# Moving the q terms behind the third head's transposes, and taking every turned probability off PSUM with ScalarE

## The chip, the cores and the metric

The kernel runs on one core of a Trainium2 chip. TensorE (PE, with its weight loads shown apart as PEld) multiplies and transposes and writes to the banks of PSUM; VectorE (DVE) and ScalarE (ACT) read those banks; GpSimd (POOL) works on SBUF alone; SyncE (SP) issues the DMAs. The metric is the device time of one execution in microseconds. Of three runs before the change the median was 2974.68 us (2971.85 to 2978.81).

## The reference

It is one transformer block: adaptive layer norm, attention with relative positions in both q and k, and a mixture of experts. Sixteen batches of 512 rows, 256 wide, 16 heads of 16 columns, all float32.

```python
scores = jnp.einsum('bhqd,bhkd->bhqk', q, k)
dist_idx = pos_l - pos_r + M - 1          # below 0 it wraps, past the end it clamps
pos_emb = dist_emb[dist_idx]
rel_q = jnp.einsum('bhld,lrd->bhlr', q, pos_emb)
rel_k = jnp.einsum('bhrd,lrd->bhlr', k, pos_emb)
probs = softmax((scores + rel_q + rel_k) / sqrt(D))
ctx = einsum('bhqk,bhkd->bhqd', probs, v)
h = layernorm(ctx @ Wo + bo + hidden_states) * ln_gamma + ln_beta
x = x + ga * h
# then: layer norm, modulation, router, top 2 of 8 experts, sum of their outputs, residual
```

`rel_q` and `rel_k` cost the most. They are computed apart from the scores, block by block, written to DRAM, and read back as the start value of the scores.

## The kernel before

A prologue normalizes the input, projects q, k and v, and computes the first ten blocks of relative terms. Then come 64 units. A unit is one tile of 128 query rows of one batch; it handles its 16 heads in four groups (g = 0 to 3) of four heads each. Beside its own attention a unit does parts of other work: the block of relative terms that is needed ten units later (q terms in the unit itself, k terms from its last slots into the next unit), and the tail of earlier units (projection, layer norm, routing, experts). The last ten units have no such block to compute.

The order is written out by hand. A unit is 16 slots, four for each group; `at(slot, order, fn, ...)` files a piece of work under a slot and an order in it, and the last loop of the kernel emits everything by slot and order. The tile context is in manual-schedule mode, so each engine's queue is exactly that order; the framework adds the semaphores and gives out the buffers. What stands in a group's four slots on TensorE, with the names used later:

- slot 0: the first head's four transposes (`turn`, line 669, tile pt), then the next group's scores (`content`, line 644, tile qk, one bank for each of four heads). In g = 0 the expert biases (line 821, fpb) follow.
- slot 1: the second head's transposes, in g = 1 two more of the tail (line 719, pct), then the context product of the group before (line 687, pc), then the q terms (`q_set`, line 165, tile pq, four banks), in g = 3 the router (line 791, fpl).
- slot 2: the third head's transposes, then a pair of experts (line 830, fpy).
- slot 3: the k terms (`k_set`, line 186, tile pk, four banks), the fourth head's transposes, and one more piece of the tail: line 702 (pcl), 730 and 735 (ph), 778 (fpt) or 813 (fpmt), for g = 0 to 3.

One call of `q_set` is 8 matmuls, each on 32 rows of the array, so that four of them run side by side, and each of the four row groups has a bank of its own; the profile has two records for each matmul. The k terms and the scores work in the same way.

Who reads the banks: VectorE adds the scores to the relative terms and takes the maximum (line 650), adds the k terms in place (line 195), copies the first head's transposes (line 674) and takes one expert of each pair (line 841). ScalarE copies the transposes of the second to fourth head (line 672) and the q terms (line 175), does the exponentials (line 660, two heads in slot 2 and two in slot 3, for the next group), and the other expert of a pair (line 845, ye). All TensorE output but the context's goes through one pool of seven banks (`ps`, tag g), and a tile waits until the last reader of the bank it gets is done. In the program's own order a tile mostly gets the bank that was used seven tiles before.

Of the kernel before, what the change touches and what calls it, by code (L numbers as in the profile page):

```python
# [34 lines left out]
def adaln_attention_moe_kernel(  # L35
# [34 lines left out]
    nc = tc.nc  # L70
# [51 lines left out]
    def bank(name):  # L122
        return ps.tile([P, S], F32, tag="g", name=name)


    class Rel:
# [7 lines left out]
        @staticmethod  # L134
        def at(n):
            s, m = n // 32, n % 32
            return s, m // 8, m % 8 // 2, m % 2
# [70 lines left out]
    rel = Rel()  # L208


    with ExitStack() as pro:
# [205 lines left out]
        with tc.tile_pool(name="setup", bufs=1) as su:  # L417
# [34 lines left out]
            for cc in range(NE):  # L452
                pt = bank(f"scT_{cc}")[:, 0:NB]
# [207 lines left out]
                t_["s", g][:, t, :], t_["s", g][:, t, :], AF.Exp, bias=t_["m", g][:, t : t + 1]  # L661
            )

    def turn(u, g, t, on_act):
        t_ = units[u]
        pt = bank(f"pt_{u}_{g}_{t}")
        for rb in range(NL):
            cols = slice(rb * P, (rb + 1) * P)
            nc.tensor.transpose(pt[:, cols], t_["s", g][:, t, cols], ident)  # L669
        pT = tp.tile([P, S], F32, tag="pT", name=f"pT_{u}_{g}_{t}")  # L670
        if on_act:
            nc.scalar.copy(pT, pt)  # L672
        else:
            nc.vector.tensor_copy(pT, pt)  # L674
        t_["p", g, t] = pT

    def context(u, g):
# [190 lines left out]
    for u in range(NP):  # L868
        z = 16 * u
        for g in range(4):  # L870
            q0 = z + 4 * g
            at(q0 - 12, 0, load_scores, u, g)
            at(q0 - 4, 5, content, u, g)
            at(q0 - 2, 7, exps, u, g, (0, 1))
            at(q0 - 1, 7, exps, u, g, (2, 3))
            for t in range(4):
                at(q0 + t, 3, turn, u, g, t, t > 0)
            at(q0 + 5, 4, context, u, g)
        at(z - 16, 0, lambda u: units.setdefault(u, {}), u)
        at(z - 13, 0, load_k, u, 0)  # L880
        at(z - 6, 0, load_k, u, 1)
        at(z - 15, 0, load_q, u)
        at(z - 7, 0, mask_q, u)
        at(z - 9, 0, load_rest, u)
        at(z + 15, 0, load_tail, u)
        z += 16
        at(z + 3, 6, back, u)
        at(z + 5, 3.5, contextT, u)
        at(z + 7, 6, project, u)
        at(z + 8, 0, residual, u)  # L890
        at(z + 10, 0, norm2, u)
        at(z + 11, 6, modulate, u)
        at(z + 13, 7, route, u)
        at(z + 15, 7, mask_t, u)
        at(z + 16, 7, bias, u)
        for pr in range(4):
            at(z + 18 + 4 * pr, 6, experts, u, pr)
            at(z + 19 + 4 * pr, 1, expert_sums, u, pr)
        at(z + 35, 0, finish, u)

        z -= 16
        n = u + LEAD
        if n < NP:
            for g in range(4):
                at(z + 1 + 4 * g, 6, rel.q_set, n, g)
                at(z + 15 + 4 * g, 2, rel.k_set, n, g)
            for g in range(4):
                at(z + 28 + 2 * g, 0, rel.store, n, g)
        if n + 1 < NP:
            for w in rel.wants(n + 1):  # L910
                o = 8 + w[3] if w[0] == "q" else (16, 17, 21, 25)[w[2] % 2 * 2 + w[3]]
                at(z + o, 0, rel.load, w)
# [52 lines left out]
```

## Time and profile before

| | before |
|---|---|
| median of 3 runs | 2974.68 us |
| profiled execution | 2971.56 us |
| its span, first to last instruction | 2969.8 us |
| TensorE clock granted, mean | 0.971 |
| distance of units that compute q terms | 40.05 us |
| distance of most of the last ten units | 28.5 us |
| DMA moved over the span | 268 GB/s |

The span is divided so: some 500 us of prologue, about 2120 us with units that also compute relative terms, the rest with units that don't. In the middle of the run the granted clock is full. A record of TensorE ends where the profile models its end, so records can be longer than the work in them; the chain of waits follows the last instruction back to what held it, and gives the time between one end and the next.

### The profile page before, as it was taken

To read this page: it belongs to the slowest core of one execution; us is meant where nothing else is said; L and a number is where in the kernel's file an instruction comes from. 1 tells how busy PE (TensorE), PEld (TensorE's weight loads), DVE (VectorE), ACT (ScalarE), POOL (GpSimd) and SP (SyncE) were. 2 spreads that over 40 slices of the span, in tenths; PEclk is the share of its full clock that TensorE was granted. 3 is DMA by queue.
4 is the path that set the end of the run, shared out by engine and by line. 5 is a ranking of instruction groups with operands and counts; after the bars stand their busy time and mean duration, and the time that the engine had idled before them with its cause. 6 is when DMAs were issued, how large, how long until landed. Compare 5 with 4: busy or idle time off the path is not lost.

```text
span 2969.8 us, 75984 instructions
## 1 busy us (share of the span) xinstructions
PE 2815.0 (95%) x30186; PEld 1845.8 (62%) x30186; DVE 1984.0 (67%) x5396; ACT 1933.7 (65%) x3682; POOL 629.8 (21%) x863
## 2 busy tenths in 40 slices
PE   8889864999999999999999999999999999999997
PEld 5556552666666666666666666666666666666564
DVE  5446542777777777777767777677777767776664
ACT  2344433777776777777677677777767777767774
POOL 1000000121222222122222212222222222222333
PEclk9889866999999999999999999999999999999999
DMA  6879997798988889988888998888898888898661
GB/s 191 302 260 319 298 302 259 229 290 268 287 269 271 280 283 293 280 272 281 272 271 277 287 281 274 268 283 277 281 295 268 286 273 272 272 280 279 211 232 54
DMA packets 855346, 796.46 MB, mean 268 GB/s; under 512 B 25545, under 2 KB 649409, under 8 KB 854737
## 3 DMA queue, kind: packets, MB, share of 16 engines
q1 hardware_dynamic: 854032, 790.03, 84.3%
q8 instruction: 240, 3.93, 0.5%
q10 hardware_dynamic: 960, 1.57, 0.2%
q14 instruction: 114, 0.93, 0.1%
HBM read 462.20 MB, written 328.25 MB: 266 GB/s over the span
## 4 chain that ended last, share of the span: by engine, by line
PE 79%; POOL 2%; DMA 1%; DVE 1%; SPq 1%; issue 1%; ACT 1%; POOLq 0%; ACTq 0%; DVEq 0%
PE pt L669 18%; PE fpy L830 14%; PE pq L165 13%; PE qk L644 12%; PE pc L687 8%; PE pk L186 8%; PE ph L735 2%; PE fpl L791 1%; PE pcl L702 1%; POOL qm L614 1%; DMA vu<-v_d 1%; PE fpt L778 1%; PE fpb L821 0%; PE pct L719 0%; POOL rstd L101 0%
## 5 line engine op out<-in xcount | busy, mean ns | idle before, releaser
L175 ACT COPY r<-pq 128x512 f32<-128x512 f32 x1024 | 525.4, 603 | 385.8 <-PE pq L165 368.9
L195 DVE TENSOR_TENSOR r<-pk,r 128x512 f32<-128x512 f32 x1024 | 635.0, 683 | 192.8 <-PE pk L186 187.3
L660 ACT ACTIVATE s<-s,mx 128x512 f32<-128x512 f32 x1024 | 691.6, 735 | 50.2 <-DVE mx L654 47.2
L650 DVE CUSTOM_DVE_ANT_0 s<-qk,s 128x512 f32<-128x512 f32 x1024 | 644.0, 685 | 39.2 <-PE qk L644 36.7
L669 PE MATMUL pt<-ident,s 128*128 128x128 f32 x4096 | 652.0, 283 | 10.7 <-ACT s L660 10.3
L669 PEld LDWEIGHTS pt<-ident,s 128*128 128x128 f32 x4096 | 451.0, 142 | 289.3 <-issue 77.7
L672 ACT COPY pT<-pt 128x512 f32<-128x512 f32 x768 | 459.5, 598 | 252.1 <-PE pt L669 250.4
L851 POOL TENSOR_TENSOR ye<-ye,ye 128x256 f32<-128x256 f32 x192 | 140.6, 732 | 1633.0 <-ACT ye L845 1627.5
L830 PE MATMUL fpy<-we_sb,fhT 128*128 128x512 f32 x1024 | 483.4, 595 | 0.0
L165 PE MATMUL pq<-t_r,qe 32*128 32x256 f32 x4096 | 467.1, 417 | 4.0 <-DMA qe<-eq_d 2.9
L644 PE MATMUL qk<-k,qm 32*128 32x512 f32 x2048 | 388.9, 644 | 28.0 <-POOL qm L614 28.0
L186 PEld LDWEIGHTS pk<-t_f,ke 32*128 32x128 f32 x8192 | 268.8, 190 | 189.1 <-ACT pT L672 157.7
L841 DVE SCALAR_TENSOR_TENSOR fy<-fpy,fmask,fy 128x256 f32<-128x256 f32 x256 | 123.8, 483 | 384.6 <-PE fpy L830 375.6
L165 PEld LDWEIGHTS pq<-t_r,qe 32*128 32x128 f32 x4096 | 283.3, 186 | 143.1 <-DVE mx L650 67.8
L186 PE MATMUL pk<-t_f,ke 32*128 32x128 f32 x8192 | 321.2, 288 | 7.2 <-DVE r L195 3.4
L687 PE MATMUL pc<-pT,vu 128*32 128x128 f32 x8192 | 278.2, 277 | 0.0
L830 PEld LDWEIGHTS fpy<-we_sb,fhT 128*128 128x128 f32 x1024 | 175.4, 191 | 124.9 <-issue 124.9
L687 PEld LDWEIGHTS pc<-pT,vu 128*32 128x32 f32 x8192 | 209.2, 110 | 43.5 <-issue 42.9
L644 PEld LDWEIGHTS qk<-k,qm 32*128 32x128 f32 x2048 | 141.5, 183 | 104.6 <-DVE r L195 47.3
L674 DVE COPY pT<-pt 128x512 f32<-128x512 f32 x256 | 174.5, 682 | 24.9 <-PE pt L669 20.3
L101 POOL TENSOR_TENSOR rstd<-rstd,mhalf 128x1 f32<-128x1 f32 (+1 forms) x144 | 88.0, 611 | 438.5 <-DVE rstd L100 434.9
L845 ACT ACTIVATE ye<-fpy,fmask 128x256 f32<-128x256 f32 x256 | 127.5, 498 | 45.2 <-DVE fy L841 45.1
(111 smaller groups left out, 2175.6 us busy)
## 6 DMA issues: line engine op xcount, KB each, us to landing
rel_d<-r SPq DMA_DIRECT2D x256, 1024.0 KB, 8.5
s<-rel_d SPq DMA_DIRECT2D x256, 1024.0 KB, 7.8
vu<-v_d SPq DMA_DIRECT2D x64, 576.0 KB, 7.7
ke<-ek_d SPq DMA_DIRECT2D x128, 256.0 KB, 7.1
k<-k_d SPq DMA_DIRECT2D x128, 256.0 KB, 6.5
gt<-gates_d SPq DMA_DIRECT2D x64, 256.0 KB, 4.7
v_d<-v SPq DMA_DIRECT2D x16, 576.0 KB, 6.4
xt<-in_x SPq DMA_DIRECT2D x16, 512.0 KB, 6.1
```

The source lines that it names most:

```text
L165: nc.tensor.matmul(bs[t][:, a * 256 : (a + 1) * 256], e[32 * t : 32 * t + 32, (g % 2) * 2 + a, :], t_r[32 * t : 32 * t + 32, :, m0 : m0 + RK],
L175: nc.scalar.copy(dst[:, t], bs[t].rearrange("p (a c) -> p a c", a=2))
L186: nc.tensor.matmul(bs[t][:, a * 128 : (a + 1) * 128], e[32 * t : 32 * t + 32, a, :], t_f[32 * t : 32 * t + 32, :, m0 : m0 + LQ], start=Tru ...
L195: nc.vector.tensor_tensor(dst, bs[t].rearrange("p (r l) -> p l r", r=8), dst, ALU.add)
L644: nc.tensor.matmul(bs[t], t_["q"][rows, pa, cc, :], t_["k", cc][rows, :], start=True, stop=True)
L650: nc.vector.tensor_tensor_reduce(st[:, t, :], bs[t], st[:, t, :], 0.25, -3.0e38, ALU.add, ALU.max, mx[:, t : t + 1],)
L660: nc.scalar.activation(t_["s", g][:, t, :], t_["s", g][:, t, :], AF.Exp, bias=t_["m", g][:, t : t + 1])
L669: nc.tensor.transpose(pt[:, cols], t_["s", g][:, t, cols], ident)
L672: nc.scalar.copy(pT, pt)
L674: nc.vector.tensor_copy(pT, pt)
L687: nc.tensor.matmul(pc[32 * t : 32 * t + 32, g, :], t_["v"][:, rb, h * VW : h * VW + 32], pTs[t][:, rb * P : (rb + 1) * P], start=(rb == 0) ...
L830: nc.tensor.matmul(py, t_["hT"][:, kc, :], we_sb[:, kc, pr * 2 * E : (pr + 1) * 2 * E], start=(kc == 0), stop=(kc == NE - 1),)
```

## The change

The q terms of a group move from slot 1, order 6 to slot 2, order 4: from behind the context product to behind the third head's transposes (order 3 in slot 2) and ahead of the experts (order 6). The copy of the first head's transposes moves from VectorE to ScalarE, so that `turn` has one form for all four heads. With that, the pool gives out its banks in another order.

```diff
-    def turn(u, g, t, on_act):
+    def turn(u, g, t):
...
         pT = tp.tile([P, S], F32, tag="pT", name=f"pT_{u}_{g}_{t}")
-        if on_act:
-            nc.scalar.copy(pT, pt)
-        else:
-            nc.vector.tensor_copy(pT, pt)
+        nc.scalar.copy(pT, pt)
         t_["p", g, t] = pT
...
             for t in range(4):
-                at(q0 + t, 3, turn, u, g, t, t > 0)
+                at(q0 + t, 3, turn, u, g, t)
...
             for g in range(4):
-                at(z + 1 + 4 * g, 6, rel.q_set, n, g)
+                at(z + 2 + 4 * g, 4, rel.q_set, n, g)
                 at(z + 15 + 4 * g, 2, rel.k_set, n, g)
```

ScalarE's order in a group becomes: copies of the first, second and third head, four q-term copies, two exponentials, ye, the copy of the fourth head, two exponentials. Before, the q-term copies stood between the second and the third head's copy. VectorE's order is the same but for the missing copy.

## The prediction, made before the change was run

> **What bounds the kernel now.** I read the busy row and the groups on the page first, then stretches of the run, then the chain of waits over one unit, and last VectorE's timeline inside that unit.
>
> ```profile
> PE 2815.0 (95%) x30186; PEld 1845.8 (62%) x30186; DVE 1984.0 (67%) x5396; ACT 1933.7 (65%) x3682; POOL 629.8 (21%) x863
> ...
> L672 ACT COPY pT<-pt 128x512 f32<-128x512 f32 x768 | 459.5, 598 | 252.1 <-PE pt L669 250.4
> ...
> L674 DVE COPY pT<-pt 128x512 f32<-128x512 f32 x256 | 174.5, 682 | 24.9 <-PE pt L669 20.3
> ```
>
> Three copies in four of the transposed probabilities run on ScalarE (598 ns), the fourth on VectorE (682 ns). TensorE looks full. The stretch of units that carry q terms, and the stretch after it:
>
> ```profile
> 501.60:2623.80 2122.20, 2117.39 (x24237) 1388.04 (x24229) 1514.13 (x4069) 1518.65 (x2918) 489.46 (x671) 1.00 0.88 276
> 2623.80:2950.00 326.20, 300.90 (x3022) 194.92 (x3018) 215.31 (x669) 222.16 (x423) 106.49 (x147) 0.99 0.64 214
> ```
>
> Columns: window, its length, busy PE, PEld, DVE, ACT, POOL, clock, DMA share, GB/s. A unit takes 40.05 us with q terms (the distance of line 702's transposes from unit to unit) and 28.5 without. PE is 100% "busy", weight loads 65%. The chain of waits, two groups of heads (start, length, what):
>
> ```profile
> 1513.53 1.01 PE pc L687 x32
> 1514.54 1.08 PE pq L165 x16
> 1515.62 0.54 PE fpl L791 x4
> 1516.16 0.49 PE pt L669 x4
> 1516.65 1.72 PE fpy L830 x4
> ...
> 1522.77 1.01 PE pc L687 x32
> 1523.78 1.86 PE pq L165 x16
> 1525.64 0.59 PE pt L669 x4
> 1526.22 1.72 PE fpy L830 x4
> ```
>
> The same 16 q-term records take 1.08 us in one group and 1.86 in the next. In the unit's four groups (g = 0 to 3) they take 1.86, 1.83, 2.52 and 1.08, so 0.78 + 0.75 + 1.44 = 2.97 us are waiting inside "busy". VectorE shows what for, here in g = 0:
>
> ```profile
> 1521.95 0.68 DVE L674 COPY pT<-pt 128x512 f32<-128x512 f32 x1
> 1522.54 0.68 DVE L650 CUSTOM_DVE_ANT_0 s<-qk,s 128x512 f32<-128x512 f32 x1
> ...
> 1523.15 0.69 DVE L650 CUSTOM_DVE_ANT_0 s<-qk,s 128x512 f32<-128x512 f32 x1
> ...
> 1523.76 0.69 DVE L650 CUSTOM_DVE_ANT_0 s<-qk,s 128x512 f32<-128x512 f32 x1
> ```
>
> By the built program the last of the four q-term banks takes over the bank that the third of these score reads frees, at 1524.45. The q terms end at 1525.64, 1.19 later; in g = 1 and g = 2 the same distance is 1.18 and 1.19 (1534.59 to 1535.77; 1505.27 to 1506.46). A late last bank thus costs a whole q set (1.08) after it.
>
> **What the Trainium skill says.** "Perfetto Trace Analysis", section Identifying the Most-Contended Engine: busy time of matmuls is no measure of headroom; weight-load share is. The trace agrees (100% against 65%). Same page, Optimization Strategy: "Consistent bubbles" can mean that PSUM runs out for the next tile; here they sit inside the records, by the bank read at 1524.45. Same page, Optimizing Scalar/DVE Operations: fixed access to PSUM costs ScalarE less (about 51 ns against 125); the trace agrees, 598 ns against 682. "TensorE: Matmul & The Clock Gate", The mechanism: matmuls start and end in program order, so one q term without a bank holds all that follows; here nothing overtakes the 1.86.
>
> **The change part by part.** *Copies.* 256 copies leave VectorE, 256 enter ScalarE. On VectorE a copy holds the next read back 0.59 to 0.60 us (1521.95 to 1522.54). All score reads of a group come 0.59 earlier, since the copy was followed at once by them and the score matmuls are done (in g = 0 the next point shows by how much). On ScalarE one adds some 0.5, 2.0 a unit: 28.6 of 40.05 becomes 30.6 of about 39 (78%). It stands there behind the second pair of exponentials, ends 0.5 to 1.2 us after VectorE's last k add, and the first q-term bank, its new user, is asked for 2.2 us or more after that add (1521.95+0.08 to 1523.78+0.59): hidden. If that cover went, each us late would hold all q terms.
>
> *Order on TensorE.* Before: context (pc), q terms, third transposes (pt), experts (fpy). After: pc, pt, q terms, fpy, k terms. Nothing is added; SP's queue and POOL's have the same instructions in the same order, and the stores of r, three slots after the k terms, read what the q copies of two units later overwrite, which only gain a slot.
>
> *Banks.* The new build gives the last q bank the fourth score read in g = 0, 1 and 3, the third in g = 2; before it was the third, third, second and second. So one more read (0.61) stands ahead, one copy (0.59) less. Releases: g = 0, 1525.06 − 0.59 = 1524.47; g = 1, 1535.20 − 0.59 = 1534.61; g = 2, 1505.88 − 0.60 = 1505.28. Plus 1.19 the q terms end at 1525.66, 1535.80, 1506.47: 0.02 later than now on average. TensorE, if never held, would end them at pc's end + 0.59 + 1.08: 1525.45, 1535.61, 1505.61, all earlier, so the bank still decides. But pt (0.59) is then done beforehand, inside the old wait. That is the gain: 0.59 a group in three groups.
>
> *What goes against it.* fpy now follows q terms (32-row tiles) directly. A pt after such tiles costs 0.59, after full-array work 0.44 to 0.49; so fpy may cost 0.14 more. The trace has no fpy in that place: bounds 0 and 0.15; I take 0.14. In g = 3 nothing waits (1.08), and there pc, fpl, pt, q, fpy only gain that switch: −0.14. There too ScalarE's chain behind the q copies gets tight: copies start 0.08 after q's end, exponentials 1.92 on, ye (line 845) 1.23 on, 0.50 long, 0.06 to pass on: 3.8 after q's end, while the next group's first transposes, who want that bank, could come 3.51 after it (1516.49 to 1520.00). They come 0.3 late; the score matmuls behind them already wait for k adds (0.36 after their start), so I charge 0.05.
>
> *Sum.* 3 × (0.59 − 0.14 − 0.02) − 0.14 − 0.05 = 1.10 us a unit; 54 units carry q terms: 59.4. In the ten units without them, TensorE idles 1.86 before line 778, for layer-norm work that stands behind the score reads on VectorE; those come 0.59 earlier: 5.9. The k terms' stalls in front of the score matmuls hang on k adds and move along. Together 65.3: the profiled 2971.6 becomes 2906.3. The median is 3.1 above the profiled run: **2909 us**. With the switch at 0 a unit gains 1.66 and the time is about 2879.
>
> **The rivals.**
> (a) *The q terms wait no more at all*: 54 × 2.97 = 160, some 2814. For it: the wait on VectorE's copy is gone. Against it: the last bank still hangs on a score read.
> (b) *ScalarE becomes the bound*: the 0.3 us at ye shows in every group, 1.2 a unit, and eats the gain: about 2975. For: exponentials now follow the q copies. Against: in g = 0, 1, 2 the first copies start before q's end (1525.26 against 1525.64), and more tail work lies before the next transposes.
> (c) *Slower: the score reads do not move up.* If the first read must wait for its matmul and not for VectorE, the last q bank comes 0.6 later and pays 1.19 behind it: 3 × (0.43 − 0.59) − 0.19 = −0.67 a unit, 36 us, about 3011. It decides from 0.43 us on: first score matmul done that much after the last k add. Now it is done some 0.4 before it (in g = 0: begins 1520.53, second pass 0.53 on, 0.59 long: 1521.65, the add ends 1522.03).
> (d) *DMA*: 276 GB/s at 88% would become 284 at 90%; if it could not, no change. The page shows slices of 302 and 319 GB/s, and score loads land some 8 us after issue, a good ten before use.
> That the change does not do what it says is excluded by the built order: 256 VectorE copies fewer, 256 ScalarE copies more, q terms behind pt everywhere.
>
> **How the numbers follow.** My sum 0.70 (2879 to 2930 with the unknown switch and small second waits), (a) or part of it 0.06, (b) 0.10, (d) 0.04, (c) 0.10. Range 2868 to 2950: the sum's own, plus part of (a) and of (b). Faster by over 0.2% (which is about what a measurement of this kernel can tell) 0.86, within 0.04, slower 0.10.
>
> **What would show it.** Units 38.9 us apart; q terms still 1.2 to 2 us long in three groups, ended by the score read, with pt before them; no line 674; ACT about 2070 us busy. Wrong if q terms take 1.08 everywhere, if pt of the next group waits for ye, or if fpy behind q terms takes much over 1.9.

## The result: 2934 us, faster, but by 40 us and not by 65

| | before | predicted | after |
|---|---|---|---|
| median, us | 2973.86 (4 runs) | 2909 | 2934.24 (4 runs, 2932.23 to 2937.05) |
| profiled execution / its span, us | 2971.56 / 2969.8 | 2906.3 / – | 2935.72 / 2934.0 |
| unit with q terms, us | 40.05 | 38.9 | 39.11 |
| most of the last ten units, us | 28.5 | 27.9 | 28.5 |

The ratio of after to before is 0.9859, with an interval of 0.9843 to 0.9874. The sign was right and the time lies inside the range, 2868 to 2950. It lies 4 us above the 2879 to 2930 that the prediction gave to its own sum, and both parts of the predicted gain were too large.

The page of the changed kernel, its busy row and its copies of the transposes (line numbers are three lower than before, because the branch is gone):

```profile
PE 2770.9 (94%) x30186; PEld 1803.2 (61%) x30186; DVE 1837.4 (63%) x5140; ACT 2068.8 (71%) x3938; POOL 630.1 (21%) x863
...
L671 ACT COPY pT<-pt 128x512 f32<-128x512 f32 x1024 | 595.3, 584 | 317.9 <-PE pt L669 295.3
```

All 1024 copies of transposes are ScalarE's. ScalarE gained 135.1 us (1933.7 to 2068.8; "about 2070" was predicted), VectorE lost 146.6. The two stretches that correspond to those before, columns as there:

```profile
501.60:2590.00 2088.40, 2079.29 (x24367) 1351.67 (x24368) 1401.66 (x3879) 1645.32 (x3152) 497.34 (x681) 1.00 0.89 282
2590.00:2915.00 325.00, 299.47 (x2919) 191.84 (x2918) 184.59 (x616) 234.43 (x453) 100.77 (x139) 0.97 0.64 211
```

The stretch of the q terms is shorter at an unchanged granted clock, and the DMA moves 282 GB/s in place of 276. The chain of waits (start, length, what) in a g = 0 and a g = 2 of one unit of the changed kernel, with the end of the g = 3 ahead of it:

```profile
1503.78 0.11 PE fpmt L810
1503.89 0.66 PE pt L669 x4
...
1506.62 1.01 PE pc L684 x32
1507.63 0.59 PE pt L669 x4
1508.21 1.15 PE pq L165 x16
1509.37 1.91 PE fpy L827 x4
...
1525.94 1.01 PE pc L684 x32
1526.95 0.59 PE pt L669 x4
1527.54 1.95 PE pq L165 x15
1529.49 1.91 PE fpy L827 x4
```

The transposes (pt) now stand ahead of the q terms (pq), as built. The four q sets of a unit (the q terms of one group each) take 1.16 (1.15 in the g = 0 shown), 1.26, 1.95 and 1.08 us, so 0.08 + 0.18 + 0.87 = 1.13 us are still waiting, where 2.97 were. VectorE's timeline in the g = 2 shown shows the release of the last q bank:

```profile
1526.06 0.41 DVE L750 TENSOR_SCALAR x<-x,mv,rstd 128x256 f32<-128x256 f32 x1 [0.67 <-POOL rstd L101]
1526.39 0.68 DVE L650 CUSTOM_DVE_ANT_0 s<-qk,s 128x512 f32<-128x512 f32 x1
...
1527.61 0.69 DVE L650 CUSTOM_DVE_ANT_0 s<-qk,s 128x512 f32<-128x512 f32 x1
```

The third score read of the group, that of the last line shown, ends at 1528.30, and the q terms end at 1529.49: 1.19 us later, as before the change. In g = 0 it is the fourth read, at 1508.18, and the q terms end 1.19 later too. So the releases that the prediction read from the build are the ones the profile shows. With the copy gone, what stands directly ahead of the reads of g = 2 is the scaling of the layer norm (line 750).

Where a unit's 0.94 us (40.05 − 39.11) come from, counted from the end of pc to the end of fpy:

| group | before: pq + pt + fpy | after: pt + pq + fpy | gain |
|---|---|---|---|
| g = 0 | 1.86 + 0.59 + 1.72 | 0.59 + 1.16 + 1.91 | 0.51 |
| g = 1 | 1.83 + 0.59 + 1.72 | 0.59 + 1.26 + 1.91 | 0.38 |
| g = 2 | 2.52 + 0.59 + 1.72 | 0.59 + 1.95 + 1.91 | 0.38 |
| g = 3 | 1.08 + 1.72 | 1.08 + 1.91 | −0.19 |
| g = 3 to the next g = 0: first transposes, scores, biases | 2.01 | 2.14 | −0.13 |

In the last row the transposes take 0.66 instead of 0.44, and the scores and biases behind them take 0.08 less. The rows sum to 0.95. Fifty-four units of 0.94 make 50.8 us.

The last row and the first belong together. The score reads of g = 0 follow VectorE's k adds and not these transposes (in the next unit the adds end at 1544.86, and the record of the first read begins at 1544.78). Counted from the start of fpmt, the piece ahead of the transposes in the chain, the first of them begins 1.88 us later (1503.78 to the line below); before it was 2.48 (1520.06 to 1522.54), so it moved up by 0.60.

```profile
1505.66 0.68 DVE L650 CUSTOM_DVE_ANT_0 s<-qk,s 128x512 f32<-128x512 f32 x1
```

TensorE reaches the end of pc 0.13 later (3.85 us after the start of fpmt, in place of 3.72), and the q set then waits 0.13 less for its read. Taken together, g = 0 gains 0.38, as g = 1 and g = 2 do.

The profiled executions differ by 35.8 us of span (2969.8 − 2934.0), and they split like this, by the line that transposes the context (pcl). Up to the first of them, 532.5 became 538.0: +5.5. The next 51 distances are 46.6 shorter (2038.3 to 1991.7). The last 12 are 3.1 longer (365.4 to 368.5), and what follows the last one 2.1 (33.7 to 35.8). Of the +5.5, 4.9 arise ahead of the first of a unit's transposes (492.05 and 496.95), where nothing was changed yet. In the copy alone and the move alone below, whose code up to there is the same too, that point lies at 494.05 and 492.54, and in the last kernel at 498.17. So I take the 4.9 for scatter of the prologue; no kernel was profiled twice to show it. In the last 12, three units took 30.1 in place of 28.5, each with about 3.4 us in which the granted clock was half.

### The profile page after: what moved, and what is told of

It is laid out like the page before. It is cut to its first block, busy times and chain, and to the rows that moved or that the text cites. A ratio compares the mean times of both kernels' runs of the same rounds, so it can differ in the third digit from the quotient of the medians.

```text
span 2934.0 us, 76492 instructions
## 1 busy us (share of the span) xinstructions
PE 2770.9 (94%) x30186; PEld 1803.2 (61%) x30186; DVE 1837.4 (63%) x5140; ACT 2068.8 (71%) x3938; POOL 630.1 (21%) x863
## 4 chain that ended last, share of the span: by engine, by line
PE 77%; DMA 2%; POOL 2%; DVE 1%; SPq 1%; ACT 1%; issue 1%; POOLq 0%; DVEq 0%; ACTq 0%
PE pt L669 18%; PE fpy L827 15%; PE qk L644 12%; PE pq L165 10%; PE pc L684 8%; PE pk L186 8%; PE ph L732 2%; DMA vu<-v_d 1%; PE fpl L788 1%; PE pcl L699 1%; PE fpb L818 1%; PE fpt L775 1%; POOL qm L614 1%; PE pct L716 0%; POOL rstd L101 0%
## 5 line engine op out<-in xcount | busy, mean ns | idle before, releaser
L671 ACT COPY pT<-pt 128x512 f32<-128x512 f32 x1024 | 595.3, 584 | 317.9 <-PE pt L669 295.3
L669 PE MATMUL pt<-ident,s 128*128 128x128 f32 x4096 | 660.0, 284 | 10.8 <-ACT s L660 10.4
L827 PE MATMUL fpy<-we_sb,fhT 128*128 128x512 f32 x1024 | 506.1, 617 | 0.0
L644 PE MATMUL qk<-k,qm 32*128 32x512 f32 x2048 | 380.1, 650 | 28.0 <-POOL qm L614 28.0
L165 PE MATMUL pq<-t_r,qe 32*128 32x256 f32 x4096 | 370.5, 409 | 4.2 <-DMA qe<-eq_d 2.8
L165 PEld LDWEIGHTS pq<-t_r,qe 32*128 32x128 f32 x4096 | 240.2, 186 | 82.4 <-issue 41.7
L644 PEld LDWEIGHTS qk<-k,qm 32*128 32x128 f32 x2048 | 133.4, 184 | 101.5 <-DVE r L195 47.6
L614 POOL TENSOR_SCALAR qm<-qs,par 128x256 f32<-128x256 f32 x128 | 117.7, 932 | 150.1 <-DMA k<-k_d 137.8
```

The lines of the kernel that those rows point to most:

```text
L165: nc.tensor.matmul(bs[t][:, a * 256 : (a + 1) * 256], e[32 * t : 32 * t + 32, (g % 2) * 2 + a, :], t_r[32 * t : 32 * t + 32, :, m0 : m0 + RK],
L614: nc.gpsimd.tensor_scalar(qm[:, pa], qs, par[:, pa : pa + 1], None, ALU.mult)
L644: nc.tensor.matmul(bs[t], t_["q"][rows, pa, cc, :], t_["k", cc][rows, :], start=True, stop=True)
L827: nc.tensor.matmul(py, t_["hT"][:, kc, :], we_sb[:, kc, pr * 2 * E : (pr + 1) * 2 * E], start=(kc == 0), stop=(kc == NE - 1),)
```

## The experiments

Two theories. **The bank theory**, the prediction's own: the copy on VectorE and the order of reads decide when the last q bank is free, the q set ends about 1.19 us after that, and everything else is a matter of adding up. Then the two edits can be priced apart from the chain alone. **The rival**: the gain is another one (ScalarE's earlier copies, or the DMA), or ScalarE is what now stands in the way, so that a kernel with the copy alone would be no better than the whole change.

**The copy alone.** The q terms stay where they were:

```diff
-                at(q0 + t, 3, turn, u, g, t, t > 0)
+                at(q0 + t, 3, turn, u, g, t, True)
```

> Edit: only the first head's copy goes to ScalarE, the q terms stay in slot 1. Theory 1 (the last q-term bank and the score read that frees it decide, and a q set takes 1.19 us after that read): the build gives the last q bank the third score read in g = 0 and 1 and the second in g = 2, as before, and these come 0.59 us earlier, so the q terms take about 1.27, 1.25, 1.92 and 1.08 us, the experts 1.72, a unit 40.05 - 1.78 = 38.3 us, and the time is about 2878 us: more than the whole change gains. Theory 2 (the gain is that of pulling the third transposes into the wait): the copy alone does little, a unit stays near 40 us and the time within 10 us of before.

It took 2884.08 us (2882.63 to 2885.59), ratio 0.9691 with an interval of 0.9675 to 0.9707: 50 us better than the whole change, and 6 above the time expected. A unit is 38.26 us, as expected, and its q sets are 1.26, 1.24, 1.92 and 1.08. The chain of waits in its g = 0:

```profile
1520.56 1.01 PE pc L687 x32
1521.57 1.26 PE pq L165 x16
1522.83 0.59 PE pt L669 x4
1523.42 1.72 PE fpy L830 x4
```

The q set shrank from 1.86 by 0.60, the length by which the copy had held back each read, and fpy stays at 1.72. The three waiting groups shrink by 0.60 + 0.59 + 0.60 = 1.79, and the unit by 40.05 − 38.26 = 1.79. ScalarE does every copy here too (2044.9 us busy), so ScalarE isn't what costs the whole change its gain.

**The move alone.** The copy stays on VectorE:

```diff
-                at(z + 1 + 4 * g, 6, rel.q_set, n, g)
+                at(z + 2 + 4 * g, 4, rel.q_set, n, g)
```

> Edit: only the q terms move to slot 2, the first head's copy stays on VectorE. Theory 1: the built banks make the q terms wait for the third score read in g = 0, 1 and 2 and the fourth in g = 3, with VectorE's copy still ahead of the reads; with the transposes ahead of them and 0.19 us for the experts' switch a group gains 0.40, 0.40, loses 0.21 and 0.19, and the bank that ye frees costs 0.09: a unit takes about 39.7 us, the time about 2957 us. Theory 2 (the move makes the gain): a unit near 39.1 us, about 2934 us.

It took 2958.77 us (2954.95 to 2965.1), ratio 0.9951, interval 0.9933 to 0.9969. A unit is 39.70 us: the move brings 0.35. The chain in its g = 2:

```profile
1536.31 0.59 PE pt L669 x4
1536.90 2.54 PE pq L165 x15
1539.44 1.91 PE fpy L830 x4
```

Here pt stands ahead, inside the old wait, and the q set still takes 2.54 where it took 2.52. The reason is in VectorE's reads of this group, of which this is the third:

```profile
1537.57 0.69 DVE L650 CUSTOM_DVE_ANT_0 s<-qk,s 128x512 f32<-128x512 f32 x1
```

It ends at 1538.26 and the q terms end 1.18 after it, where before it was the second. One read more (0.61) takes back the transposes' 0.59. In g = 0 and 1 it is the third read as before, and the sets fall to 1.16 and 1.25. So the gains are 0.51, 0.39, −0.21 and −0.19, and −0.13 at the next first transposes (0.65 here): 0.37, against 0.35 measured.

The parts give 1.79 and 0.35, the whole 0.94. They don't add up because both draw on the same wait. With the copy gone, the waits of g = 0 and g = 1 are down to 0.18 and 0.16 (1.26 − 1.08, 1.24 − 1.08), and pt's 0.59 can no longer fit into them unless the last bank comes later; and it does come one read later (fourth for third, third for second). In g = 2 some 0.84 is left, which pt could fill, and the later read takes that back too. What is left of the move is its cost: 0.19 a group at fpy, and some 0.02 where a read of 0.61 takes the place of a pt of 0.59. From the copy alone to the whole change the groups lose 0.22 (g = 0 with the transposes ahead of it, 0.09 + 0.13), 0.21, 0.22 and 0.19; that sums to 0.84, and the units differ by 0.85.

**The copy, with idle work in its place on VectorE.** This asks whether time ahead of the reads is paid one to one, whoever spends it. Two operations on scratch tiles, whose results nobody uses, take the copy's place in VectorE's queue. No part of the computation is left out.

```diff
...
+        if t == 0:
+            nc.vector.tensor_tensor(spare, spare, spare, ALU.max)
+            nc.vector.tensor_tensor(idle, idle, idle, ALU.max)
...
-                at(q0 + t, 3, turn, u, g, t, t > 0)
+                at(q0 + t, 3, turn, u, g, t, True)
```

> Edit: the copy alone, plus two idle operations of VectorE on its own small tiles (192 and 128 elements, some 0.45 us by the length of its 256-element operations) in the place that its copy had, ahead of the score reads. No bank has another reader than in the copy alone. Theory 1 (the gain is VectorE's time ahead of the score reads): the q terms grow back by 0.45 us in three groups, to about 1.7, 1.7, 2.4 and 1.1, a unit from 38.27 to 39.6 us, the time to about 2957 us. Rival (the gain comes from which engine frees the transposes' bank): nothing changes, 38.27 us a unit, 2884 us.

It took 3035.36 us (3029.5 to 3041.06), ratio 1.0194, interval 1.0174 to 1.0213. A unit is 40.92 us and not the expected one, since the operations took longer than I had estimated, and not equally long in each group. VectorE's timeline around the g = 0, g = 1 and g = 2:

```profile
1501.41 0.82 DVE L678 TENSOR_TENSOR idle<-idle 128x128 f32<-128x128 f32 x1
...
1511.96 0.29 DVE L678 TENSOR_TENSOR idle<-idle 128x128 f32<-128x128 f32 x1
...
1523.17 0.81 DVE L678 TENSOR_TENSOR idle<-idle 128x128 f32<-128x128 f32 x1
```

The same operation takes 0.29 us or 0.82. GpSimd's timeline has what differs:

```profile
1501.35 0.73 POOL L863 TENSOR_TENSOR fy<-fy,x 128x256 f32<-128x256 f32 x1
...
1523.07 0.77 POOL L762 TENSOR_TENSOR x<-x,gt 128x256 f32<-128x256 f32 x1 [0.53 <-DVE x L761]
```

In both slow cases a GpSimd operation had begun just before, and VectorE's ended 0.14 to 0.15 us after that one's end (1502.23 after 1502.08; 1523.98 after 1523.84). This is what the Trainium skill describes, "SBUF — State Buffer", section Who interferes with whom: "A DVE instruction with two SBUF inputs contends with a GpSimd instruction that reads SBUF", and the order of issue decides which of the two is blocked. The trace agrees: among 200 such operations between 560 and 2600 us, the 99 that overlap with one of GpSimd took 0.81 to 0.83 us, the other 101 took 0.28 to 0.29. For the question at hand the miss helps, because it gives three different delays. The reads were pushed back by 1.19, 0.47 and 1.01 us, and the q sets took 2.45, 1.71 and 2.92: 1.19, 0.47 and 1.00 more than with the copy alone. The chain has it in g = 0, where the copy alone had 1.26:

```profile
1502.80 2.44 PE pq L165 x16
```

The three sum to 2.66, and 38.26 + 2.66 is the unit's 40.92. So each microsecond ahead of the score reads goes into the q set whole.

**The last units.** The prediction had credited them with 0.59 each, and it came only in the last distance of all (25.70 to 25.11). In the changed kernel the layer norm's result (xn) releases TensorE's transposes (fpt), and the wait is 1.87 us. TensorE's line, and GpSimd's timeline ahead of it:

```profile
2742.92 0.44 PE L775 MATMUL fpt<-ident,xn 128*128 128x128 f32 x2 [1.87 <-DVE xn L765]
...
2739.32 0.73 POOL L753 TENSOR_TENSOR x<-x,xu 128x256 f32<-128x256 f32 x1
2740.03 1.85 POOL L614 TENSOR_SCALAR qm<-qs,par 128x256 f32<-128x256 f32 x2
2741.85 0.56 POOL L101 TENSOR_TENSOR rstd<-rstd,mhalf 128x1 f32<-128x1 f32 x1
```

The power that the layer norm needs (line 101) was ready to run: VectorE had finished its input at 2740.99. It stands in GpSimd's queue behind the mask of a later unit's q (line 614, 1.85 us), and VectorE waits 1.46 us for it. The edit on top of the changed kernel files the mask three slots earlier:

```diff
-        at(z - 7, 0, mask_q, u)
+        at(z - 10, 1, mask_q, u)
```

> Edit: the changed kernel, with GpSimd's masking of q three slots earlier (slot z-10 in place of z-7). Theory (the last ten units gain nothing from earlier score reads since GpSimd does the mask of 1.85 us ahead of the second layer norm's power): in those units line 775's transposes come 0.77 us earlier, the wait before them falls from 1.87 to about 1.1 us, units of 28.5 become 27.7, units with q terms stay at 39.1, and the time falls by about 8 us to 2926 us. Rival (another piece of the layer norm's chain takes the place): units stay at 28.5 us and the time at 2934 us.

It took 2924.6 us (2924.39 to 2927.08), ratio 0.9831, interval 0.9815 to 0.9848, some 10 us less than the whole change. The last units are 27.73 us. TensorE's timeline shows what is left of the wait:

```profile
2738.26 0.44 PE L775 MATMUL fpt<-ident,xn 128*128 128x128 f32 x2 [1.09 <-DVE xn L765]
```

1.09 in place of 1.87 is 0.78 a unit, and 28.5 − 27.73 = 0.77. The units with q terms stay at 39.13, and none of the last units takes 30.1. One unit at the changeover from one kind of unit to the other takes 34.06 us (30.49 in the changed kernel). GpSimd's timeline in it shows a new wait:

```profile
2644.96 1.83 POOL L614 TENSOR_SCALAR qm<-qs,par 128x256 f32<-128x256 f32 x2 [13.19 <-DMA qs<-q_d]
```

The earlier mask comes up ahead of its q. It waits for the load, and the power of the first layer norm, queued behind it, begins only at 2647.43. TensorE then waits 1.91 us at a head's transposes until a score read is done, and 3.19 for xn, where the changed kernel has 2.27 for xn alone.

**Both that help.** The copy alone, with the early mask, and without the move:

```diff
-                at(q0 + t, 3, turn, u, g, t, t > 0)
+                at(q0 + t, 3, turn, u, g, t, True)
...
-        at(z - 7, 0, mask_q, u)
+        at(z - 10, 1, mask_q, u)
```

> Edit: the copy alone and GpSimd's mask three slots earlier, q terms in slot 1. Theory (the two are independent): a unit with q terms 38.27 us, without 27.7 us, about 2875 us.

It took 2879.63 us (2879.06 to 2883.18), ratio 0.9674, interval 0.9658 to 0.969, with units of 38.29 and 27.73 us. The sizes of the units add up as expected; the total gains 4.5 us over the copy alone, because a changeover unit of 35.72 takes back part: its mask, too, waits for the load of q, and TensorE's two waits are 3.76 and 3.19 us.

**The next thing ahead of the reads.** With the copy gone, it is g = 2's layer-norm scaling (the line 750 shown above) that keeps the reads late. On the kernel just told, the scaling is filed behind the score reads, and the second layer norm is split and moved on with it:

```diff
...
-        at(z + 8, 0, residual, u)
-        at(z + 10, 0, norm2, u)
-        at(z + 11, 6, modulate, u)
+        at(z + 8, 5.5, residual, u)
+        at(z + 11, 1.5, stats2, u)
+        at(z + 11, 2.5, norm2, u)
+        at(z + 12, 5.5, modulate, u)
```

> Edit: as copy_mask, and in g = 2 the first layer norm's scaling on VectorE (line 753), which waits 0.67 us for GpSimd, goes behind the score reads; the second layer norm is cut in two (statistics ahead of the k adds, scaling behind them) and its transposes come one slot later. Theory 1: the q terms of g = 2 fall from 1.92 to 1.08 us, the k adds start 0.3 us late, a unit takes 37.7 us and the time is about 2848 us. Rival (VectorE's work is only moved to another place on the way, the k adds): 38.2 us a unit or more, 2875 us or more.

It took 2858.49 us (2846.03 to 2862.07), ratio 0.9585, interval 0.9562 to 0.9609, the fastest of all. A unit is 37.67 us and its q sets are 1.26, 1.24, 1.08 and 1.08. VectorE's timeline in its g = 2 (the scaling is now line 753):

```profile
1530.13 0.69 DVE L650 CUSTOM_DVE_ANT_0 s<-qk,s 128x512 f32<-128x512 f32 x1
...
1530.94 0.41 DVE L753 TENSOR_SCALAR x<-x,mv,rstd 128x256 f32<-128x256 f32 x1
```

The scaling follows the group's last read, and the 0.86 us of waiting in that group are gone (1.94 to 1.08). The unit gains less, 38.29 − 37.67 = 0.62. The chain of waits in this kernel no longer stays on TensorE there: from 1528.31 to 1537.40 it runs over the score reads, the scaling, GpSimd's three residual operations, the statistics and xn. The total missed its expectation by 10 us: in its profile the first pcl lies at 538.8, and most of the last units take 28.12 to 28.15 in place of 27.73, two of them 29.7, each with 3.4 us at half the clock. Why, was not tested.

## Why the prediction was right, and where its sizes were off

**What bounded the kernel: right.** The last q bank, freed by a score read, set the end of the q terms before and after, with 1.19 to 1.20 us from release to end for every q set that waits, in some 45 steady units of each of the eight kernels. The kernel with idle work shows that the read is the cause: 1.19, 0.47 and 1.01 us of delay gave 1.19, 0.47 and 1.00.

**"0.59 − 0.14 − 0.02" in three groups: right but for the switch.** It predicted 0.43 a group, and 0.38 came in each, with the 0.13 at the transposes counted with g = 0. In g = 1 and g = 2 the q sets are what "Banks" gives: 1.83 − 0.59 + 0.61 − 0.59 = 1.26, and 2.52 − 0.60 + 0.61 − 0.59 = 1.94 (measured 1.26 and 1.95). In g = 0 the same sum gives 1.29, and 1.16 came, since TensorE arrives 0.13 later and the reads do not. The switch costs 0.19 and not 0.14.

**"fpy may cost 0.14 more": mis-sized.** It is 1.91 behind q terms against 1.72 behind pt, in all groups, with either form of the copy. The bound of 0.15 came from pt, whose 0.59 against 0.44 is the same step for another instruction; it was no bound for fpy. Each of the four groups loses 0.05 more than reckoned: 0.43 becomes 0.38 in three, and 0.14 becomes 0.19 in g = 3.

**"So I charge 0.05" for ye: right wait, and nothing to charge.** This is one of the signs that the prediction named against itself, and it came. At the end of the unit shown, ScalarE ends ye at 1542.95, and the weight loads of the next group's first transposes had waited for it:

```profile
1543.00 0.42 PEld L669 LDWEIGHTS pt<-ident,s 128*128 128x128 f32 x4 [0.29 <-ACT ye L842]
```

That is the 0.3 that was reckoned. The transposes count 0.66 in the chain instead of 0.44, the score matmuls and biases behind them give back 0.08, and the 0.13 left go into the wait of g = 0, which ends with the score read all the same. The prediction's own figures had room for it: it saw TensorE ready at 1525.45 and the bank's end at 1525.66. The same 0.65 shows with the move alone, so it comes from the move and not from ScalarE's extra copy.

The four fpy (4 × 0.05 = 0.20) and the needless charge (0.05) make 1.10 into 0.95; with the measured 0.94 it is 54 × 0.16 = 8.6 us.

**"Those come 0.59 earlier: 5.9": wrong.** The wait in the last units was put down to work behind the score reads on VectorE. It was GpSimd's queue: the releaser of VectorE's xn is the power on line 101, and that stood behind a mask of 1.85 us. Moving the mask alone took 0.78 off the wait. I had followed the wait back by one engine and stopped; the next step back was in the same view.

Of the 65.3 us predicted, 8.6 were lost in these sizes and 5.9 in the last units; 50.8 remain. The profiled execution shows 35.8. The rest lies outside the steady units: 5.5 up to the first pcl, 4.9 of it ahead of anything changed; three units that are at half clock for a while, some 4.8 (3 × 1.6); and 2.1 at the end, which goes with a longer stretch of half clock there (13.7 us against 6.8). The copy alone has two such units as well, and the same long stretch at the end; the move alone has neither. Whether the change brings the half clock about was not tested. What is left of the 15.0, some 2.6, lies chiefly at the two ends of the 54: their first distance grew by 0.40, and the last two shrank by 0.43 and 0.01, where 0.94 each had been counted.

**The rivals.** (a), q terms that wait no more, fell: 1.13 us a unit are left. (b), ScalarE as the bound, fell as a whole, since the copy alone has as many ScalarE copies and is faster; the wait for ye came, and its 0.13 went into a wait that was there anyway. (c), score reads that don't move up, fell: they moved up by 0.60 in g = 0, and the kernel was not slower. (d), the DMA, fell: the copy alone runs at 291 GB/s between 600 and 2550 us, where before ran at 279. The rival that was missing is that one edit works against the other. The working contained it already, as "one more read (0.61) stands ahead, one copy (0.59) less": it sets the move's cost against the copy's gain, and the prediction should have asked what the copy brings by itself.

## What to carry to other kernels

When a change has two edits, work out the time of each alone with the same sum as for both: here the same sum gives the copy alone 1.78 us a unit (its expectation above) and the move a loss on top of it. If several tiles share one rotating pool of banks, moving a piece of work by one place changes which reader frees its last bank, and here the length of the reads queued ahead of that one was paid in full. Follow a wait back until it reaches work that was not itself waiting; the engine named first was here only the messenger.

## What the hardware showed that was not expected

- A pair of experts (full-array matmuls) took 1.91 us directly behind matmuls on 32 rows of the array, and 1.72 behind transposes. Four transposes took 0.58 to 0.59 behind such matmuls, 0.59 also behind the expert biases and the context product, and 0.44 to 0.49 behind the router and the pieces of the tail. What makes the difference was not taken apart.
- A VectorE operation of 128 elements a partition with two inputs in SBUF took 0.29 us alone and 0.81 to 0.82 when a GpSimd operation had begun just before it; it ended 0.14 to 0.15 us after GpSimd's. The operation of 192 elements ahead of it, which in g = 2 began 0.16 to 0.17 us before GpSimd's, took 0.35 us, as it does where GpSimd is idle.
